# A four-layer graph network on one core: the last buckets of two layers by gathered rows, and fewer progress marks from TensorE

## The chip, the cores and the metric

The kernel runs on one core of a Trainium2 chip. The metric is device time in microseconds (us) of one execution. The program has four computing engines that run their own instruction streams: TensorE (PE, with its weight loads shown as PEld), VectorE (DVE), ScalarE (ACT) and GpSimd (POOL). A fifth stream, SyncE (SP), only issues transfers here. The engines know of one another only through semaphores: an instruction can add one to a semaphore when it is done (the code calls this a mark), and another engine can wait for a value.

## The reference

8192 nodes with 32 features each, 262144 edges sorted by their target node, four layers. Each layer adds a sum over incoming edges to the node's features and normalizes the result. `segment_sum` adds the rows of all edges with the same target.

```python
edge_index = jnp.stack([src, dst])
# layer 0: a 32x32 weight for each of 64 edge types
msg = einsum('ei,eio->eo', x[src], weight[etype]);  x = layernorm(x + segment_sum(msg, dst))
# layer 1: edge weight e
x = layernorm(x + segment_sum(x[src] * e[:, None], dst))
# layer 2
x = layernorm(x + segment_sum(x[src], dst))
# layer 3: a small network per edge makes four 8x8 matrices w from 32 edge features
h = relu(edge_feat @ W1 + b1);  w = (h @ W2 + b2).reshape(e, 4, 8, 8)
m = products of w with x[src] and 4 more edge features
x = layernorm(x + segment_sum(m, dst) + own part of x)
```

## The kernel before, in words

Edges are handled in tiles of 128 (one per partition), 2048 tiles in all. A group is 8 tiles (256 groups, `GG`), a quad is 4 tiles (512 quads, `NQ`). Nodes are handled in 64 blocks of 128 (`NB`), 8 blocks to a chunk for normalizing (`LC`). In the code `PE`, `V`, `A`, `G` and `S` are the five instruction streams; `X.mark(ins)` makes an instruction raise the engine's own semaphore, `X.after(...)` makes the engine wait. The order in each stream is the order of the Python code.

**Table.** First a table `fytab` of every node's row times each of the 64 weights is computed and stored to memory (line 408).

**Layer 0** (loop at `for g in range(GG + 2)`). For each group POOL gathers the 8 tiles' rows from `fytab` by indirect transfers (`gathers`, line 387, one transfer per tile, four after each half of the loop body). DVE builds a one-hot matrix of the target nodes (line 509) and splits the rows into three bf16 parts (lines 624 to 629, `parts`). PE multiplies both into a sum per window of nodes (line 662) and raises its mark. Four groups share one bank, which `bank_out` reduces (line 635). POOL fetches 12 groups ahead, and may start the next four gathers only when PE has marked the sums of the current group, and the four after that when PE has marked everything issued so far. When enough windows are ready, `windows` (line 499) and `normalize` (lines 458 to 468) produce eight blocks of new features, 8 times in the stage.

**Matrices, beside layer 0.** In the same loop `matrices(i)`, called 256 times, prepares layers 1 and 2: for 32 target nodes each call builds the columns of two dense adjacency matrices, one with edge weights (fp32, `famat`, 1 MB per call) and one with counts (bf16, `fcmat`, 0.5 MB). DVE builds one-hot matrices (lines 562, 564, 567). PE multiplies them for four units of eight nodes (line 576), each unit in two banks out of five, with a mark after every unit. ACT copies a unit's two banks to staging buffers (lines 581 and 582), which frees them. SP stores the staging buffers (lines 586 and 587) from two buffers in turn.

**Layers 1 and 2.** The matrices come back in 32 loads of 8 MB (layer 1, 2 blocks each) and 16 loads of 8 MB (layer 2, 4 blocks each) into two buffers (`bring`, line 698), each issued as one transfer when PE has marked the end of the multiplication with the buffer before. PE multiplies x with a load (lines 761 and 764), ACT copies the sums (line 770), and `turn` (line 741) folds them one load later and normalizes. `self_part` (lines 727 to 731) prepares layer 3's own part. At the end of layer 2 the rows are stored as the table `fxtab` (only there).

**Layer 3** (loop at `for q in range(NQ + LAG3 + 2)`). For each quad POOL gathers four tiles of rows from `fxtab`, eight quads ahead, each released by the mark of a quad's weights. PE computes the hidden values for two quads (line 899, `hidden`, with a mark; ACT applies relu in line 907), then the 4 x 256 weights of the quad (line 923, a mark), then the sums of the quad `LAG3` = 4 back (line 932, a mark). DVE makes the products (lines 960, 963, 967) from the weights' banks, of which there are two, builds a one-hot matrix (line 509) and reduces every second quad's sums (lines 988 to 991). Every other quad it also prepares factors (lines 863 to 870).

Of the kernel before, what the change touches and what calls it, by code (L numbers as in the profile page):

```python
# [12 lines left out]
FP = mybir.dt.float32  # L13
# [88 lines left out]
AW = 41200  # L102


@with_exitstack
def in_order(ctx: ExitStack, tc, x, a, w0, w1, b1, w2, si, keep):
# [8 lines left out]
    m["xtab"] = dram.tile([N, D], FP, name="fxtab")  # L115
# [30 lines left out]
def raw_layers(tc, x, a, w0, w1, b1, w2, si, m, bad):  # L146
# [7 lines left out]
    ytab, xtab, hist, amat, cmat = (m[k] for k in ("ytab", "xtab", "hist", "amat", "cmat"))  # L154
# [294 lines left out]
    x_st = Landing(tc, "st_x")  # L449
    ln_last = [None]  # L450

    def normalize(l, c, acc, pm, x_in, x_out, x3=None):


        ds = slice(c * LC, (c + 1) * LC)
        y, yc, sq = (lnf[:, k].rearrange("p (d f) -> p d f", f=D) for k in range(3))
        V.after(pm, ln_last[0])
        read = own(V, V.e.tensor_add(y, acc.rearrange("p (d f) -> p d f", f=D), x_in[:, ds, :]))  # L458
        own(V, V.e.tensor_reduce(lns[:, 0], y, AX.X, OP.add))
        own(V, V.e.tensor_scalar(lns[:, 1], lns[:, 0], 1.0 / D, None, op0=OP.mult))  # L460
        vm = V.mark(V.e.tensor_sub(yc, y, lns[:, 1, :, None].to_broadcast([P, LC, D])))
        A.after(vm)
        V.after(A.mark(A.e.activation(sq, yc, AF.Square)))
        A.after(V.mark(V.e.tensor_reduce(lns[:, 2], sq, AX.X, OP.add)))
        V.after(A.mark(A.e.activation(lns[:, 0], lns[:, 2], AF.Sqrt, bias=eps, scale=1.0 / D)))
        own(V, V.e.reciprocal(lns[:, 3], lns[:, 0]))
        xo = x_out[:, ds, :]
        ln_last[0] = V.mark(V.e.tensor_tensor(xo, yc, lns[:, 3, :, None].to_broadcast([P, LC, D]), op=OP.mult))
        if x3 is not None:

            r1, r2 = y, sq
            V.after(ln_last[0])
            own(V, V.e.tensor_copy(x3[:, ds, 0:D], xo))
            own(V, V.e.tensor_sub(r1, xo, x3[:, ds, 0:D]))
            own(V, V.e.tensor_copy(x3[:, ds, D:2 * D], r1))
            own(V, V.e.tensor_sub(r2, r1, x3[:, ds, D:2 * D]))
            ln_last[0] = V.mark(V.e.tensor_copy(x3[:, ds, 2 * D:], r2))
        if l == 2:
            S.after(ln_last[0])
            x_st.add(S.e.dma_start(xtab.rearrange("(d p) f -> p d f", p=P)[:, ds, :], xo))  # L480
        return read

    def windows(c, acc, free):

        d0 = c * LC
        todo = []
        for j in [0, 1, 2, 3, -2, -1, 4]:
            lo, hi = 0, LC
# [6 lines left out]
        wv = win.rearrange("p (d j) f -> p d j f", j=4)  # L495
        PE.after(*free)
        for n, (j, lo, hi) in enumerate(todo):
            g0 = 4 * (d0 + lo) + j
            ins = PE.e.matmul(acc[:, lo * D:hi * D].rearrange("p (d f) -> p d f", f=D),
                              shift[:, P - WS * j:2 * P - WS * j], wv[:, g0 // 4:g0 // 4 + hi - lo, g0 % 4, :],  # L500
                              start=(n == 0), stop=(n == len(todo) - 1))
        return PE.mark(ins)

    def ready(c):

        return min(GG, 4 * (LC * (c + 1) - 1) + 5)
# [41 lines left out]
    bank_free = {k: (acc_free[0] if k == 2 else None) for k in range(2, 7)}  # L548
    st_ld = [Landing(tc, f"st_m{k}") for k in range(2)]
    w_up = [None]  # L550
    units = [0]

    def matrices(i):
# [3 lines left out]
        if i % WB == 0:  # L557
# [6 lines left out]
        V.e.tensor_tensor(oh_l[:, b], iota[:, None, :].to_broadcast([P, 16, P]),  # L564
                          meta_l[:, pp, k0:k0 + 16, None].to_broadcast([P, 16, P]), op=OP.is_equal)
        wo = (i % WB) * 16
        vm = V.mark(V.e.tensor_tensor(oh_k[:, b, :, 1, :], oh_k[:, b, :, 0, :],
                                      w_ps[:, wo:wo + 16, None].to_broadcast([P, 16, 64]), op=OP.mult))
        PE.after(vm)
        for q in range(4):  # L570
            bk = [2 + (2 * units[0] + h) % 5 for h in range(2)]
            PE.after(*(bank_free[b5] for b5 in bk))
            for j in range(4):
                for h in range(2):
                    hs_ = slice(64 * h, 64 * h + 64)
                    ins = PE.e.matmul(bank[:, bk[h], :].rearrange("p (c s j) -> p c s j", s=64, j=4)[:, :, :, j],  # L576
                                      oh_l[hs_, b, 4 * q + j, :], oh_k[hs_, b, 4 * q + j], start=True, stop=True)
            pm = PE.mark(ins)
            A.after(pm, st_ld[b].mark() if q == 0 and st_ld[b].n else None)
            for h in range(2):  # L580
                A.e.activation(st_c[:, b, q, h], bank[:, bk[h], 0:256], AF.Copy)  # L581
                bank_free[bk[h]] = am = A.mark(A.e.activation(st_a[:, b, q, h], bank[:, bk[h], 256:512], AF.Copy))  # L582
            units[0] += 1
        oh_used[b] = pm
        S.after(am)
        st_ld[b].add(S.e.dma_start(amat[:, 2048 * i:2048 * (i + 1)], st_a[:, b].rearrange("p u h c -> p (u h c)")))
        st_ld[b].add(S.e.dma_start(cmat[:, 2048 * i:2048 * (i + 1)], st_c[:, b].rearrange("p u h c -> p (u h c)")))

# [4 lines left out]
    agg_free = [freed[0], freed[0]]  # L593
# [6 lines left out]
    per = 4  # L600
# [31 lines left out]
    def bank_out(n):  # L632

        V.after(sums_of[per * n + per - 1])
        agg_free[n % 2] = vm = V.mark(V.e.tensor_reduce(
            win[:, per * n:per * (n + 1), :], bank[:, n % 2, 0:per * 3 * D].rearrange("p (g c f) -> p g f c", c=3, f=D),
            AX.X, OP.add))
        return vm
# [5 lines left out]
    for g in range(GG + 2):  # L644
        if g >= 2 and (g - 2) % per == per - 1:
            vm = bank_out((g - 2) // per)
            while done < NB // LC and ready(done) <= g - 1:
                acc = bank[:, (g - 2) // per % 2, 0:LC * D]
                agg_free[(g - 2) // per % 2] = vm = normalize(0, done, acc, windows(done, acc, (vm,)), x_a, x_b)
                done += 1  # L650
        if g >= GG:
            continue
        h, bk, c = g % NO, (g // per) % 2, g % per
        if g == FIRST // 2:
            V.after(slots(), x_in)
        V.after(oh_free[h])
        one_hot(oh[:, h], g * GT, GT)
        PE.after(parts(g))
        if c == 0:
            PE.after(agg_free[bk])  # L660
        for t in range(GT):
            ins = PE.e.matmul(bank[:, bk, 3 * c * D:3 * (c + 1) * D], oh[:, h, t, :],  # L662
                              xp[:, g % 4, t].rearrange("p c f -> p (c f)"), start=(t == 0), stop=(t == GT - 1))
        oh_free[h] = sums_of[g] = PE.mark(ins)
        fetch_rows(g + AHEAD, 0, sums_of[g])
        if g >= FIRST:
            upto = min(CB, (g - FIRST + 1) * CB // (GG - FIRST - 4))
            while made < upto:
                matrices(made)
                made += 1  # L670
        fetch_rows(g + AHEAD, 1, now(PE))
# [9 lines left out]
    z = cut(NB, D)  # L681
    zx = cut(2, P)
    end = (now(PE), now(V), now(A), *stored)
# [5 lines left out]
    seq = [(1, c) for c in range(32)] + [(2, c) for c in range(16)]  # L689
    land = {}  # L690

    def bring(n):
        if n < len(seq):
# [3 lines left out]
            if l == 1:  # L697
                land[n] = m_ld[b].add(S.e.dma_start(buf[b], amat[:, c * 16384:(c + 1) * 16384]))
            else:
                land[n] = m_ld[b].add(S.e.dma_start(buf[b].bitcast(BF), cmat[:, c * 32768:(c + 1) * 32768]))  # L700

    bring(0)
    bring(1)
# [14 lines left out]
    own_part = [None]  # L718

    def self_part(j):  # L720
        xv = x_b[:, 4 * j:4 * j + 4, :].rearrange("p d f -> p (d f)")
        u = j % 2
        if j == 0:
# [5 lines left out]
        PE.after(A.mark(A.e.activation(zx[:, u], bank[:, 4 + u, 0:P], AF.Copy)), zf[1 - u])  # L729
        V.after(PE.mark(PE.e.matmul(bank[:, 6, 0:P], zx[:, u], sis, start=True, stop=True)))  # L730
        zf[u] = V.mark(V.e.tensor_add(z[:, 4 * j:4 * j + 4, :].rearrange("p d f -> p (d f)"), bank[:, 6, 0:P], xv))

    def turn(l, c, n, am):
# [10 lines left out]
        if d0 + nb == LC:  # L744
            out_free[o] = normalize(l, c * nb // LC, bank[:, 2 + o, 0:LC * D], pm, x_b if l == 1 else x_a,
                                    x_a if l == 1 else x_b, x3 if l == 1 else None)
            outs[0] += 1

    for n, (l, c) in enumerate(seq):
        b = n % 2  # L750
        nn = 256 if l == 1 else 512
        if n == 32:
            turn(*pend)
            pend = None
            PE.after(ln_last[0])
# [19 lines left out]
        if l == 2 and c >= 3 and c % 2 == 1:  # L775
            self_part(c - 3)
            self_part(c - 2)
# [3 lines left out]
    self_part(NB // 4 - 2)  # L781
    self_part(NB // 4 - 1)
# [19 lines left out]
    LAG3 = 4  # L802
# [23 lines left out]
    G.after(x_st.mark())  # L826
# [15 lines left out]
    def fetch_rows(q):  # L842

        if q < NQ:
            G.after(quad.get(q - AHEAD, {}).get("w"))
            rows[q // 2] = gathers(xtab, src, q // 8, q % 8 * 4, 4)
# [45 lines left out]
    def hidden(q):  # L892
# [9 lines left out]
        pm = PE.mark(ins)  # L902
        if q % 8 == 6:
            ef_free[k] = pm
# [9 lines left out]
    hidden(0)  # L914
    for q in range(NQ + LAG3 + 2):

        if q % 2 == 0 and q + 2 < NQ:
            hidden(q + 2)
        if q < NQ:
            k, wp = w_bank()  # L920
            PE.after(quad[q]["h"], w_free[k])
            for t in range(4):
                ins = PE.e.matmul(wp[:, t, :], hs[0:65, q % 4, t * P:(t + 1) * P], w2_s[0:65], start=True, stop=True)  # L923
            quad[q]["w"] = PE.mark(ins)
            quad[q]["k"] = k, wp
            fetch_rows(q + AHEAD)
# [544 lines left out]
```

## Time and profile before

| | us |
|---|---|
| median of 3 runs | 7502.81 (7498.84 to 7513.8) |
| the profiled execution | 7590.36 |
| its span, first to last instruction | 7588.5 |

The span by stage, each stage cut at the first or last instruction of its kind:

| stage | us | PE | DVE | ACT | POOL | PE clock | DMA share |
|---|---|---|---|---|---|---|---|
| table, start of layer 0 (0 to 435.6) | 435.6 | 186 | 118 | 165 | 214 | 0.63 | 0.56 |
| layer 0 and the matrices (to 3533.7) | 3098.1 | 1914 | 2097 | 1219 | 1816 | 0.67 | 0.55 |
| layers 1 and 2 (to 4521.0) | 987.3 | 581 | 55 | 37 | 0 | 0.77 | 0.98 |
| layer 3 (4531.2 to the end) | 3057.3 | 2725 | 2099 | 357 | 1943 | 0.90 | 0.12 |

The engine columns are busy microseconds, the clock is the share of full speed that TensorE was granted, and the DMA share is the mean busy share of the core's 16 DMA engines. A line of the timeline reads: start, length, engine, line of the kernel, instruction, what it writes and reads, count, and in brackets the idle time of the engine before it and what ended it. "Issue" there means that nothing in the profile ended it; "remote" means that a semaphore rose and the profile can't tell by whom. In the chain of waits, "DMA a<-b" is a transfer from its issue to its landing. The start of a matmul is recorded, while its end is modelled. Not every rise of a semaphore and not every matmul is in the record.

### The profile page before, as it was taken

To read this page: it belongs to the slowest core of one execution; us is meant where nothing else is said; L and a number is where in the kernel's file an instruction comes from. 1 tells how busy PE (TensorE), PEld (TensorE's weight loads), DVE (VectorE), ACT (ScalarE), POOL (GpSimd) and SP (SyncE) were. 2 spreads that over 40 slices of the span, in tenths; PEclk is the share of its full clock that TensorE was granted. 3 is DMA by queue.
4 is the path that set the end of the run, shared out by engine and by line. 5 is a ranking of instruction groups with operands and counts; after the bars stand their busy time and mean duration, and the time that the engine had idled before them with its cause. 6 is when DMAs were issued, how large, how long until landed. Compare 5 with 4: busy or idle time off the path is not lost.

```text
span 7588.5 us, 89476 instructions
## 1 busy us (share of the span) xinstructions
PE 5411.7 (71%) x34036; PEld 3845.9 (51%) x34036; DVE 4372.1 (58%) x9246; ACT 1780.4 (23%) x4886; POOL 3972.9 (52%) x4174
## 2 busy tenths in 40 slices
PE   7236566666666666665454778999998889889988
PEld 2125555555555555554222445555555555555555
DVE  3246666666666766665000016666767666676666
ACT  5224343333333443433000001111111111111110
POOL 3656565666565666651000006666666666666664
PEclk7556666666666666667777888989999998989898
DMA  9226555555555555557999971111111111111111
GB/s 350 87 67 146 136 144 137 150 136 144 142 139 143 144 150 136 146 135 265 432 431 431 393 303 21 24 24 24 24 24 24 24 24 24 24 24 24 25 24 21
DMA packets 290757, 999.52 MB, mean 132 GB/s; under 512 B 99022, under 2 KB 175887, under 8 KB 250639
## 3 DMA queue, kind: packets, MB, share of 16 engines
q1 hardware_dynamic: 155742, 916.89, 33.1%
q0 software_dynamic: 134144, 73.67, 9.4%
q8 instruction: 272, 4.46, 0.3%
q10 hardware_dynamic: 432, 3.15, 0.2%
q14 instruction: 167, 1.36, 0.1%
HBM read 521.39 MB, written 471.99 MB: 131 GB/s over the span
## 4 chain that ended last, share of the span: by engine, by line
PE 43%; another core or an unknown queue 17%; DVE 15%; DMA 10%; ACT 9%; issue 5%; POOL 1%; SPq 0%; DVEq 0%; ACTq 0%; POOLq 0%
PE bank L576 14%; PE bank L932 11%; PE bank L923 10%; DMA f_arena<-famat 6%; ACT f_arena L582 4%; ACT f_arena L581 4%; DVE f_arena L967 3%; DMA f_arena<-fcmat 3%; PE bank L899 2%; PE bank L761 2%; DVE f_arena L963 2%; DVE f_arena L509 2%; PE bank L764 2%; PE bank L408 1%
## 5 line engine op out<-in xcount | busy, mean ns | idle before, releaser
L387 POOL DMA_INDIRECT f_arena<-fxtab,f_src x2048 | 1942.9, 949 | 2132.7 <-PE bank L730 1077.1
L387 POOL DMA_INDIRECT f_arena<-fytab,f_row x2048 | 1961.8, 958 | 1286.5 <-issue 548.2
L576 PE MATMUL bank<-f_arena 64*128 64x128 f32 x16384 | 1626.3, 374 | 894.9 <-ACT f_arena L582 567.9
L576 PEld LDWEIGHTS bank<-f_arena 64*128 64x128 f32 x16384 | 1519.4, 280 | 989.5 <-ACT f_arena L582 477.4
L932 PE MATMUL bank<-f_arena 128*128 128x344 f32 x4096 | 1420.3, 491 | 28.6 <-issue 28.4
L923 PE MATMUL bank<-f_arena 65*128 65x256 f32 x4096 | 1107.2, 417 | 207.6 <-DVE f_arena L967 194.8
L581 ACT ACTIVATE f_arena<-bank 128x256 bf16<-128x256 f32 x2048 | 817.5, 399 | 1847.6 <-remote 1024.0
L923 PEld LDWEIGHTS bank<-f_arena 65*128 65x128 f32 x4096 | 808.2, 204 | 603.6 <-DVE f_arena L967 297.2
L932 PEld LDWEIGHTS bank<-f_arena 128*128 128x128 f32 x4096 | 856.3, 209 | 447.9 <-issue 149.0
L907 ACT ACTIVATE f_arena<-bank,f_arena 64x512 f32<-64x512 f32 x512 | 351.0, 686 | 2564.8 <-remote 1156.7
L582 ACT ACTIVATE f_arena<-bank 128x256 f32<-128x256 f32 x2048 | 828.6, 405 | 0.0
L562 DVE TENSOR_TENSOR f_arena<-bank,f_arena 128x1024 f32<-128x1024 f32 x256 | 313.3, 1224 | 806.2 <-remote 630.8
L509 DVE TENSOR_TENSOR f_arena<-bank,f_rel 128x512 f32<-128x512 f32 (+1 forms) x768 | 659.7, 859 | 139.9 <-ACT f_arena L541 127.9
L960 DVE TENSOR_TENSOR f_arena<-bank,f_arena 128x256 f32<-128x256 f32 x512 | 214.1, 418 | 836.6 <-remote 368.6
L564 DVE TENSOR_TENSOR f_arena<-bank,f_arena 128x2048 f32<-128x2048 f32 x256 | 586.6, 2291 | 8.8
L967 DVE TENSOR_TENSOR f_arena<-bank,f_arena 128x256 f32<-128x256 f32 x1536 | 550.7, 413 | 0.0
L761 PE MATMUL bank<-f_arena,f_x_b 128*32 128x256 f32 x4096 | 296.7, 461 | 332.6 <-DMA f_arena<-famat 332.6
L662 PE MATMUL bank<-f_arena 128*128 128x96 bf16 x2048 | 273.4, 261 | 364.8 <-issue 230.5
L662 PEld LDWEIGHTS bank<-f_arena 128*128 128x128 bf16 x2048 | 150.7, 120 | 484.4 <-issue 361.5
L761 PEld LDWEIGHTS bank<-f_arena,f_x_b 128*32 128x32 f32 x4096 | 146.2, 132 | 472.0 <-DMA f_arena<-famat 307.3
L458 DVE TENSOR_TENSOR f_lnf<-bank,f_x_b 128x256 f32<-128x256 f32 x8 | 3.4, 425 | 606.0 <-PE bank L741 606.0
L963 DVE TENSOR_TENSOR f_arena<-bank,f_arena 128x512 f32<-128x512 f32 x512 | 348.4, 681 | 0.0
(133 smaller groups left out, 3684.9 us busy)
## 6 DMA issues: line engine op xcount, KB each, us to landing
famat<-f_arena SPq DMA_DIRECT2D x256, 1024.0 KB
fcmat<-f_arena SPq DMA_DIRECT2D x256, 512.0 KB
fytab<-f_arena SPq DMA_DIRECT2D x64, 1024.0 KB
f_arena<-fytab,f_row POOLq DMA_INDIRECT x2048
f_arena<-fxtab,f_src POOLq DMA_INDIRECT x2048
f_arena<-laid_ea SPq DMA_DIRECT2D x64, 512.0 KB
f_arena<-laid_ea SPq DMA_DIRECT2D x64, 64.0 KB
f_arena<-laid_xT ACTq DMA_DIRECT2D x1, 1024.0 KB, 8.8
```

What stands on the lines that cost most here:

```text
L387: return G.e.indirect_dma_start(out=dest, out_offset=None, in_=table, in_offset=bass.IndirectOffsetOnAxis(ap=ix, axis=0))
L509: return V.e.tensor_tensor(o, iota[:, None, :].to_broadcast([P, n, P]), rel[:, t:t + n, None].to_broadcast([P, n, P]), op=OP.is_equal)
L564: V.e.tensor_tensor(oh_l[:, b], iota[:, None, :].to_broadcast([P, 16, P]), meta_l[:, pp, k0:k0 + 16, None].to_broadcast([P, 16, P]), op=OP ...
L576: ins = PE.e.matmul(bank[:, bk[h], :].rearrange("p (c s j) -> p c s j", s=64, j=4)[:, :, :, j], oh_l[hs_, b, 4 * q + j, :], oh_k[hs_, b, 4 ...
L581: A.e.activation(st_c[:, b, q, h], bank[:, bk[h], 0:256], AF.Copy)
L582: bank_free[bk[h]] = am = A.mark(A.e.activation(st_a[:, b, q, h], bank[:, bk[h], 256:512], AF.Copy))
L662: ins = PE.e.matmul(bank[:, bk, 3 * c * D:3 * (c + 1) * D], oh[:, h, t, :], xp[:, g % 4, t].rearrange("p c f -> p (c f)"), start=(t == 0), ...
L761: ins = PE.e.matmul(bank[q * D:(q + 1) * D, b, 0:256].rearrange("p (u h j) -> p u h j", h=2, j=4), x_b[:, s, :], mv[:, s], start=(s < 4), ...
L923: ins = PE.e.matmul(wp[:, t, :], hs[0:65, q % 4, t * P:(t + 1) * P], w2_s[0:65], start=True, stop=True)
L932: ins = PE.e.matmul(bank[:, g % 2, 0:MW], oh[:, c % NO, t, :], p[:, c % NP, t, :], start=(c % 2 == 0 and t == 0), stop=(c % 2 == 1 and t = ...
L963: V.e.tensor_tensor(pq[:, :, 0:128].rearrange("p t (o k) -> p t o k", k=16), wp[:, :, 0:128].rearrange("p t (o k) -> p t o k", k=16), a0[: ...
L967: ins = V.e.tensor_tensor(pq[:, :, 128 + 64 * mm:192 + 64 * mm].rearrange("p t (o i) -> p t o i", i=8), wp[:, :, 192:256].rearrange("p t ( ...
```

## The change

The change has these parts. Line numbers are those of the profile before.

1. **Gathered rows in layers 1 and 2.** The last 10 of 64 blocks of layer 1 and the last 4 of layer 2 (`HB`) are no longer computed from matrices. `matrices` is called 240 times in place of 256, and the last 24 of these build no `famat` part. The features after layers 0 and 1 are stored as tables too (`xtabs`; SP waits for `normalize`). In layer 1, 42 groups, and in layer 2, 18 groups of edges are gathered from these tables (`h_fetch`, at most four groups ahead, each waiting for the landing of the group two before), multiplied by the edge weight in layer 1, and summed through fp32 one-hot matrices (`h_sums`, two marks of PE per group). `h_turn` spreads them over the loads: after each load's multiplication it does the groups that are due, and calls `windows` and `normalize` for up to four blocks.
2. **Loads in pieces.** Layer 1 has 27 loads and layer 2 has 15. Each 8 MB load is issued as eight transfers of 1 MB.
3. **Fewer marks in layer 0.** `matrices` marks after every second unit, and units go through six banks (three pairs) in place of five. The mark for a group's sums is dropped where matrices follow: the first mark of `matrices` stands for both. POOL's first four gathers wait for that mark, the other four for the last. All groups use bank 0 for their sums, and a reduction after each group (`sums_out`, after the next group's one-hot and parts on DVE) takes the place of one for every four.
4. **One mark per quad in layer 3.** In each round PE does the hidden values, then the sums of the quad `LAG3` = 5 back, then the quad's weights, and marks once at the end. The hidden values' relu on ACT (`nonlinear`) waits for that mark.
5. The own part for layer 3 follows the blocks as they are finished, in whatever order.

```diff
+HB = {1: 10, 2: 4}
+MADE = {l: CB - 4 * HB[l] for l in (1, 2)}
...
-        if l == 2:
+        if l < 3:
             S.after(ln_last[0])
-            x_st.add(S.e.dma_start(xtab.rearrange("(d p) f -> p d f", p=P)[:, ds, :], xo))
+            x_st[l].add(S.e.dma_start(xtabs[l].rearrange("(d p) f -> p d f", p=P)[:, ds, :], xo))
...
+    def banks_of(u):
+        return [1 + (2 * u + h) % 6 for h in range(2)]
...
+            if q % 2 == 0:
+                continue
             pm = PE.mark(ins)
-            A.after(pm, st_ld[b].mark() if q == 0 and st_ld[b].n else None)
-            for h in range(2):
-                A.e.activation(st_c[:, b, q, h], bank[:, bk[h], 0:256], AF.Copy)
-                bank_free[bk[h]] = am = A.mark(A.e.activation(st_a[:, b, q, h], bank[:, bk[h], 256:512], AF.Copy))
-            units[0] += 1
+            marks.append(pm)
+            A.after(pm, st_ld[b].mark() if q == 1 and st_ld[b].n else None)
+            for u in range(2):
+                bk = banks_of(units[0] - 2 + u)
+                for h in range(2):
+                    ins = A.e.activation(st_c[:, b, q - 1 + u, h], bank[:, bk[h], 0:256], AF.Copy)
+                    if both:
+                        ins = A.e.activation(st_a[:, b, q - 1 + u, h], bank[:, bk[h], 256:512], AF.Copy)
+                    bank_free[bk[h]] = am = A.mark(ins)
...
+        if g:
+            agg_free = sums_out(g - 1)
...
+        PE.after(agg_free)
         for t in range(GT):
-            ins = PE.e.matmul(bank[:, bk, 3 * c * D:3 * (c + 1) * D], oh[:, h, t, :],
-                              xp[:, g % 4, t].rearrange("p c f -> p (c f)"), start=(t == 0), stop=(t == GT - 1))
-        oh_free[h] = sums_of[g] = PE.mark(ins)
-        fetch_rows(g + AHEAD, 0, sums_of[g])
+            ins = PE.e.matmul(bank[:, 0, 0:3 * D], oh[:, h, t, :], xp[:, g % 4, t].rearrange("p c f -> p (c f)"),
+                              start=(t == 0), stop=(t == GT - 1))
+        marks = []
         if g >= FIRST:
-            upto = min(CB, (g - FIRST + 1) * CB // (GG - FIRST - 4))
+            upto = min(MADE[2], (g - FIRST + 1) * MADE[2] // (GG - FIRST - 4))
             while made < upto:
-                matrices(made)
+                marks += matrices(made)
                 made += 1
-        fetch_rows(g + AHEAD, 1, now(PE))
+        if not marks:
+            marks.append(PE.mark(ins))
+        oh_free[h] = sums_of[g] = marks[0]
+        fetch_rows(g + AHEAD, 0, marks[0])
+        fetch_rows(g + AHEAD, 1, marks[-1])
...
+            for k in range(8):
+                o = buf[b][:, 2048 * k:2048 * (k + 1)]
+                if l == 1:
+                    land[n] = m_ld[b].add(S.e.dma_start(o, amat[:, c * 16384 + 2048 * k:c * 16384 + 2048 * (k + 1)]))
...
+    def h_fetch(l, g):
+        if g >= GG:
+            return
+        k = count["got"] % 4
+        count["got"] += 1
+        G.after(x_st[l - 1].mark() if g == HG[l] else None, hx_free[k], hl.get((l, g - 2), (0, None))[1])
+        for t in range(GT):
+            mk = h_ld[k].add(indirect(hx[:, k, t, :], xtabs[l - 1][:, :], src[:, g * GT + t:g * GT + t + 1]))
+        hl[l, g] = k, mk
...
+                V.after(hoh_free[r])
+                PE.after(V.mark(one_hot(hoh[:, r], g * GT + 4 * hh, 4)))
+                for t in range(4):
+                    ins = PE.e.matmul(bank[:, 6, (g - g0) * D:(g - g0 + 1) * D], hoh[:, r, t, :], hx[:, k, 4 * hh + t, :],
+                                      start=(hh == 0 and t == 0), stop=(hh == 1 and t == 3))
+                hoh_free[r] = hx_free[k] = PE.mark(ins)
+            h_fetch(l, g + 4)
...
+        h_turn(l, HG[l] + (GG - HG[l]) * c // (chunks[l] - 1))
...
-    LAG3 = 4
+    LAG3 = 5
...
-            quad[q]["w"] = PE.mark(ins)
             quad[q]["k"] = k, wp
-            fetch_rows(q + AHEAD)
...
+        if q < NQ + LAG3:
+            pm = PE.mark(ins)
+        if q < NQ:
+            quad[q]["w"] = pm
+            fetch_rows(q + AHEAD)
+        if 0 <= c < NQ:
+            quad[c]["a"] = pm
+        if q % 2 == 0 and q + 2 < NQ:
+            nonlinear(q + 2, pm)
```

## The prediction

> **What bounds the kernel now.** I read the page's group list first, then the idle times before POOL, then POOL, ACT, PE and DVE in order of time inside one group and one quad, and last the chain of waits through layers 1 and 2.
>
> ```profile
> span 7588.5 us, 89476 instructions
> ...
> L387 POOL DMA_INDIRECT f_arena<-fxtab,f_src x2048 | 1942.9, 949 | 2132.7 <-PE bank L730 1077.1
> L387 POOL DMA_INDIRECT f_arena<-fytab,f_row x2048 | 1961.8, 958 | 1286.5 <-issue 548.2
> ```
>
> No engine is full over the span, so the bound has to be found stage by stage. Two stages hold 4,096 gathers. In both, POOL goes through them at a fixed beat and then stops. Layer 0, POOL in order of time (start, length, instruction, idle before it in brackets):
>
> ```profile
> 2113.18 0.95 POOL L387 DMA_INDIRECT f_arena<-fytab,f_row  x1 [0.30 <-issue]
> 2114.43 0.94 POOL L387 DMA_INDIRECT f_arena<-fytab,f_row  x1 [0.30 <-issue]
> 2117.62 0.94 POOL L387 DMA_INDIRECT f_arena<-fytab,f_row  x1 [2.25 <-PE bank L662]
> ```
>
> The beat is 0.95 + 0.30 = 1.25 us. Eight gathers (one group, starts 2105.68 to 2114.43) are followed by a stop of about 2.25 us that a mark of PE ends: 8 x 1.252 + 1.92 more than the beat = 11.94 us per group. In layer 3 the same view shows 12 gathers (three quads) and a stop of 2.74: 17.4 us, 5.8 per quad. So POOL is the bound of both stages, plus a stop that waits for a mark of PE.
>
> Why do the marks keep POOL waiting? They come late. ACT (L581, L582 copy one unit out of its banks) and PE in the same group:
>
> ```profile
> 2106.09 4.58 PE L576 MATMUL bank<-f_arena 64*128 64x128 f32 x48 [0.41 <-ACT f_arena L582]
> 2113.66 2.08 PE L576 MATMUL bank<-f_arena 64*128 64x128 f32 x16 [2.99 <-issue]
> ```
>
> ```profile
> 2109.01 0.40 ACT L582 ACTIVATE f_arena<-bank 128x256 f32<-128x256 f32 x1
> 2112.86 0.38 ACT L581 ACTIVATE f_arena<-bank 128x256 bf16<-128x256 f32 x1 [3.44 <-remote]
> ...
> 2117.23 0.38 ACT L581 ACTIVATE f_arena<-bank 128x256 bf16<-128x256 f32 x1 [3.16 <-PE bank L576]
> ```
>
> Units one to three (48 matmul records) end by 2110.67. ACT begins the second at 2112.86 and the third at 2117.23, 6.6 us after its matmuls. In layer 3, PE's L923 of one quad ends at 5509.9 and DVE's L960, which waits for its mark, starts at 5517.04 after 5.33 us of idling. Between late marks lie about 4.3 us while POOL gathers, and several come at once when POOL has stopped. Where no gather is issued they are prompt: after the last layer 0 gather (3453.2) DVE runs without idling:
>
> ```profile
> 3457.39 1.22 DVE L562 TENSOR_TENSOR f_arena<-bank,f_arena 128x1024 f32<-128x1024 f32 x1
> 3465.47 1.22 DVE L562 TENSOR_TENSOR f_arena<-bank,f_arena 128x1024 f32<-128x1024 f32 x1
> 3473.57 1.22 DVE L562 TENSOR_TENSOR f_arena<-bank,f_arena 128x1024 f32<-128x1024 f32 x1
> ```
>
> That is 8.09 us per group against 11.94. Likewise layer 3's last quads (7527.9 to 7537.2) take 4.65 each, PE without a pause. Layers 1 and 2 are bound by their loads:
>
> ```profile
> 3657.35 9.74 PE bank L761 x128
> 3667.11 28.87 DMA f_arena<-famat
> ...
> 4206.62 16.79 PE bank L764 x64
> 4223.42 26.43 DMA f_arena<-fcmat
> ```
>
> Layer 1's DMA share is 1.00 at 430 GB/s; PE works about 9.5 of 19.3 us per chunk there, and 16 of 21.6 in layer 2.
>
> **Part 1: fewer marks (layers 0 and 3).** What can be won is POOL's stops. Layer 0: from the first gather after the prefetch (435.6) to the last (3453.2) are 3018 us for 1920 gathers, 1920 x 1.252 = 2404 of them at the beat: 614 us of stops. Layer 3: 4531.2 to 7528.8 are 2998 us for 2048 gathers, 2564 at the beat: 434.
>
> A rule that speaks against counting on this: the Trainium skill's TensorE page ("TensorE: Matmul & The Clock Gate", "The cost: per-tile semaphore tail") gives an increment 26.3 ns. The change drops about 3 of 5 per group and 1.5 of 2.5 per quad, 244 x 3 + 512 x 1.5 = 1500, an estimate of 40 us by the rule. The row above has a mark late by 6.6 us and POOL stopped 2.25 us per group, so I go by the row: the limit is 1048 us.
>
> Layer 0 new: marks m0 (sums and units 0, 1) and m1 (units 2, 3). POOL waits for m0 before its first four gathers and m1 before the other four. With one late mark per 4.3 us the two need 8.6 us, under POOL's 10.0. The new loops: unit 3 needs ACT's four copies of unit 0, 0.27 us apart, so 1.1 us after m0 arrives; with six banks that is short. DVE now stops for m0(g-1) in sums_out(g-1), ahead of the one-hots of g (L562, L564, L567: 4.7 us), and PE's sums of g wait for sums_out (single bank 0). That loop is 0.2 + 4.7 + about 3.1 (32 of the 48 records in 4.58) + lateness, 8 us plus up to 4.3. DVE's own work is 8.09 + about 0.3 for a reduction per group in place of one per four. Ends: 10.0 (POOL alone) and 12.3 (every m0 fully late). I take 10.5, near POOL's row, as a mark early in a streak comes promptly (unit one here). 240 x 10.5 + the 80 us now between the last gather and the first load = 2600; the start (a mark kept from 457.7 to 486.2 there) is left, 30 us: 2630 against 3098, **-470**. The 16 dropped calls of matrices spare the groups that now make two; they and the lighter last 24 calls sit inside this. x_st stores of layer 0 make SP wait seven times for normalize, behind them the stores of the next matrices: cover is two buffers, a group; nothing, at most 7 x 8 = 56 us without it.
>
> Layer 3 new: hidden, sums of q-5, weights of q, one mark. PE's free pace is 4.65, DVE's 4.02, POOL's 5.01; one mark per 5 us against 4.3 possible. Hidden's ACT (two of 0.69) now waits to the end of PE's round, but its result is wanted a round later, and sums with lag 5 take values from two rounds earlier. Ends: 5.01 and 5.86 (now). I take 5.2: 512 x 5.2 + 60 = 2722 against 3057, **-335**.
>
> **Part 2: gathered rows (layers 1 and 2).** Removed: 5 of 32 and 1 of 16 loads of 8.39 MB: 352 for 402.7 MB, at 430 GB/s 117 us. Added: 60 groups x 8 gathers of 1.25 = 600 us of POOL, which idled 1077 us here. A gather's 1 KB packets take 0.10 us of each DMA engine in layer 3 and 0.22 beside layer 0's stores: 480 x 0.10 to 0.22 = 48 to 106 us of a full DMA. PE gets 16 matmul records per group at about 0.2 us (the 128-column fp32 weight loads of L741 take 0.19), 3.3 us, 1.6 groups per layer 1 chunk (5 us into 9.8 of slack), 1.3 per layer 2 chunk (4 into 5). DVE, nearly idle here, gets about 1.8 us per group. In turn marks become late here too: in layer 2 a late matmul mark holds back the next load on SP. The last store of x1 for layer 2's gathers queues on SP behind loads: 10 to 40 us once. The cut of each 8 MB load into eight is the second rule against the change: "DMA: Bandwidth & Descriptors", "Measured", has 1 MB at 341 GB/s and 16 MB at 425, which would be 1032 against 828 us for 352 MB, a loss of 200. But those are lone transfers; here eight queue at once. The row: packets of 8 KB (layer 0 stores) took 0.32 us, those of 64 KB 2.43, 408 against 432 GB/s: at worst 47 us. Sum: -117 + 77 + 20 (queue) + 0 to 47, between -60 and +80; I take **-20**.
>
> **Sum.** 7588.5 - 470 - 335 - 20 = 6763 us of span. The profiled execution (7590.4) stands 1.2% over the median 7502.8, so 6763 x 0.9885 = **6685 us**.
>
> **Rivals.** (a) POOL streams, PE's marks get later the longer the streak (one kept 28 us at 457.7), so half of the stops stay: (470 + 335) / 2 + 20 = 423, **7085**. For it: that first streak. Against: steady streaks of 12 gathers still let one through per 4.3 us. (b) The marks' number doesn't matter, only POOL: the rule's 40 us, about 90 for the double groups, 20 in part 2: **7355**. Against: the waits go through marks. (c) Slower: POOL, now tied to both marks, stops before each four gathers of layer 0: 2 x (5.01 + 1.92) = 13.9 against 12.57 on average (3018 / 240): +310, with layer 3 unchanged and part 2 at +80: 7978 x 0.9885 = **7890**. It decides from 1.3 stops per group. For it: m1 follows m0 by only one copy and one unit. Against: POOL has five microseconds of work in which m1, due after three, can arrive.
>
> **Chances.** Forecast 0.60, (a) 0.20, (b) 0.08, (c) 0.10, no change 0.02, so faster 0.88, slower 0.10. The forecast's own range is 6430 (all stops gone, part 2 at -60) to 6900; to leave no more than 2 in 10 out, 6420 to 7200. No change means within 0.2%, 15 us.
>
> **What would show it.** Right: POOL in runs of far over 12 gathers; groups at 10 to 10.8 us, quads at 5.0 to 5.3; POOL's share above 65%; layers 1 and 2 at 930 to 1030 us. Wrong: POOL idling behind PE twice per group, DVE idle before its new L635 reduction, or PE idle in layer 2 behind gathered rows.

## The result and the profile after

The changed kernel takes **7784.49 us** (median of 4 runs, 7780.85 to 7797.27) against 7500.83 for the kernel before: 1.0378 times as long, interval 1.036 to 1.0396. Forecast were 6685 us. Its profiled execution took 7797.27 us; the page begins so, and its group list has the two kinds of gathers so:

```profile
span 7795.6 us, 88905 instructions
...
L389 POOL DMA_INDIRECT f_arena<-fxtab,f_src x2528 | 2400.7, 950 | 1965.1 <-issue 705.4
L389 POOL DMA_INDIRECT f_arena<-fytab,f_row x2048 | 1957.9, 956 | 1210.3 <-issue 530.9
```

The gathers of layer 0 still leave POOL idle for 1210 us (1286 before). The stages, each from its first matmul to that of the next ("between" runs from the last matmul of layer 2 to the first of layer 3):

| us | to layer 1 | layer 1 | layer 2 | between | layer 3 |
|---|---|---|---|---|---|
| before | 3558.9 | 627.6 | 334.5 | 15.0 | 3052.5 |
| after | 3483.3 | 856.7 | 378.9 | 30.2 | 3046.5 |
| difference | -76 | +229 | +44 | +15 | -6 |

The sum, +207, is the difference of the spans. Two places differ from the forecast: layer 1 grew, and the stops did not go. By the prediction's own sum (first gather to last, less 1.252 us for each) POOL's stops fell from 614 to 531 us in layer 0 and from 434 to 425 in layer 3. First layer 3, all engines in order of time:

```profile
5493.21 1.89 PE L1041 MATMUL bank<-f_arena 65*128 65x256 f32 x8
...
5495.22 0.94 POOL L389 DMA_INDIRECT f_arena<-fxtab,f_src  x1 [0.30 <-issue]
...
5497.26 1.89 PE L1041 MATMUL bank<-f_arena 65*128 65x256 f32 x8
5498.43 0.43 DVE L1077 TENSOR_TENSOR f_arena<-bank,f_arena 128x256 f32<-128x256 f32 x1 [3.54 <-remote]
...
5498.66 0.94 POOL L389 DMA_INDIRECT f_arena<-fxtab,f_src  x1 [2.50 <-remote]
```

The weights that carry the mark end at 5495.10. DVE and POOL go on at 5498.43 and 5498.66, after 3.54 and 2.50 us of idling, while PE is already in the next quad's weights. There is one mark per quad now, and it is still late. Layer 1, then layer 2, in a table by stretches, of the kernel before and of the changed one:

```profile
core 0: us, PE busy (x) PEld busy (x) DVE busy (x) ACT busy (x) POOL busy (x), PEclk, DMA share, GB/s
3558.90:4186.50 627.60, 314.68 (x4225) 162.86 (x4226) 33.78 (x96) 18.92 (x48) 0.00 (x0) 0.73 1.00 431
4186.50:4521.00 334.50, 266.32 (x1175) 149.94 (x1175) 21.07 (x62) 18.06 (x41) 0.00 (x0) 0.89 0.93 372
```

```profile
3483.30:4340.00 856.70, 393.59 (x4297) 248.65 (x4297) 109.39 (x274) 17.85 (x47) 292.68 (x309) 0.66 0.97 273
4340.00:4719.00 379.00, 310.25 (x1360) 192.41 (x1360) 40.66 (x100) 16.69 (x39) 135.98 (x144) 0.82 0.82 316
```

In layer 1 the DMA engines are as full as before (0.97), yet move 273 GB/s in place of 431.

One thing is needed to read the experiments: the same kernel before took 7493 to 7516 us in some jobs, this comparison among them (**held** below), and 6429 to 6457 us in others (**free**), so each run is compared with the kernel before of its own job.

### The profile page after: what moved, and what is told of

Read it like the earlier page. It is cut to its first block, busy times and chain, and to the rows that moved or that the text cites. A ratio compares the mean times of both kernels' runs of the same rounds, so it can differ in the third digit from the quotient of the medians.

```text
span 7795.6 us, 88905 instructions
## 1 busy us (share of the span) xinstructions
PE 5668.1 (73%) x33318; PEld 4078.5 (52%) x33318; DVE 4389.5 (56%) x9596; ACT 1627.3 (21%) x4438; POOL 4426.6 (57%) x4654
## 4 chain that ended last, share of the span: by engine, by line
PE 46%; another core or an unknown queue 20%; DVE 10%; issue 8%; DMA 8%; ACT 6%; SPq 2%; POOL 0%; DVEq 0%; ACTq 0%; POOLq 0%
PE bank L592 16%; PE bank L1035 11%; PE bank L1041 7%; DMA f_arena<-famat 7%; PE bank L871 3%; PE bank L1007 2%; SPq L732 2%; PE bank L868 2%; ACT f_arena L1017 2%; DVE f_arena L576 2%; ACT f_arena L604 1%; ACT f_arena L602 1%; PE bank L682 1%; PE bank L410 1%
## 5 line engine op out<-in xcount | busy, mean ns | idle before, releaser
L389 POOL DMA_INDIRECT f_arena<-fxtab,f_src x2528 | 2400.7, 950 | 1965.1 <-issue 705.4
L592 PE MATMUL bank<-f_arena 64*128 64x128 f32 (+1 forms) x15360 | 1879.1, 396 | 860.5 <-issue 575.9
L592 PEld LDWEIGHTS bank<-f_arena 64*128 64x128 f32 x15360 | 1650.3, 292 | 1073.0 <-issue 754.3
L1035 PE MATMUL bank<-f_arena 128*128 128x344 f32 x4096 | 1504.6, 516 | 239.9 <-DVE f_arena L1106 131.0
L517 DVE TENSOR_TENSOR f_arena<-bank,f_rel 128x512 f32<-128x512 f32 (+1 forms) x888 | 738.2, 835 | 466.5 <-PE bank L824 293.9
L1041 PE MATMUL bank<-f_arena 65*128 65x256 f32 x4096 | 987.3, 384 | 7.3 <-issue 7.3
L604 ACT ACTIVATE f_arena<-bank 128x256 f32<-128x256 f32 x1728 | 717.1, 415 | 0.0
L658 DVE TENSOR_REDUCE f_arena<-bank 128x32 f32<-128x96 f32 x256 | 65.9, 257 | 881.9 <-remote 443.9
L576 DVE TENSOR_TENSOR f_arena<-bank,f_arena 128x2048 f32<-128x2048 f32 x240 | 549.8, 2291 | 8.2
L1007 PE MATMUL bank<-f_arena 32*64 32x512 f32 x1024 | 286.2, 635 | 72.3 <-ACT f_arena L1017 68.6
L682 PE MATMUL bank<-f_arena 128*128 128x96 bf16 x2048 | 190.3, 260 | 144.0 <-issue 57.5
```

Source lines behind the costliest of these rows:

```text
L389: return G.e.indirect_dma_start(out=dest, out_offset=None, in_=table, in_offset=bass.IndirectOffsetOnAxis(ap=ix, axis=0))
L517: return V.e.tensor_tensor(o, iota[:, None, :].to_broadcast([P, n, P]), rel[:, t:t + n, None].to_broadcast([P, n, P]), op=OP.is_equal)
L576: vm = V.mark(V.e.tensor_tensor(oh_l[:, b], iota[:, None, :].to_broadcast([P, 16, P]), meta_l[:, pp, k0:k0 + 16, None].to_broadcast([P, 16 ...
L604: ins = A.e.activation(st_a[:, b, q - 1 + u, h], bank[:, bk[h], 256:512], AF.Copy)
L1007: ins = PE.e.matmul(bank[64 * h:64 * h + 64, 2, :], w1_s[r * D:(r + 1) * D, :], ef[r * D:(r + 1) * D, k, (q % 8) // 4, :], start=True, sto ...
L1035: ins = PE.e.matmul(bank[:, g % 2, 0:MW], oh[:, c % NO, t, :], p[:, c % NP, t, :], start=(c % 2 == 0 and t == 0), stop=(c % 2 == 1 and t = ...
```

## The experiments

**The change taken apart (a free job, before 6433.69 us).** Of the changed kernel: the loads as one transfer again; and, besides that, no gathered rows (`HB = 0`), so that only the rarer marks are left. Of the kernel before: only the cut into eight.

```diff
 # e1_one_load, e3_marks_only: bring()
-            for k in range(8):
-                o = buf[b][:, 2048 * k:2048 * (k + 1)]
...
+                land[n] = m_ld[b].add(S.e.dma_start(buf[b], amat[:, c * 16384:(c + 1) * 16384]))
 # e3_marks_only also
-HB = {1: 10, 2: 4}
+HB = {1: 0, 2: 0}
 # e2_split_only: the eight pieces of the change in the kernel before
```

> The changed kernel with each load of layers 1 and 2 as one transfer of 8 MB again, gathered rows kept. Theory (the cut into eight pieces of 8 KB per partition lowers the loads from 430 to about 270 GB/s): layer 1 moves at 400 to 430 GB/s again, layers 1 and 2 take 900 to 980 us in place of about 1250, the whole about 7450 to 7530 us. Rival (the gathered rows take the bandwidth): layer 1 stays under 330 GB/s and the whole stays above 7680 us.

> The kernel before with nothing but the loads of layers 1 and 2 cut into eight pieces. Theory (the pieces): 268 MB of layer 1 at 270 GB/s are 994 us in place of 620, layer 2 about 400 in place of 350, the whole about 7900 us. Rival (the gathered rows): no difference, 7500 us within 40. Third (what the prediction had, packets of 8 KB only 5% slower): 7550 us.

> The changed kernel without gathered rows in layers 1 and 2 (all buckets are matrices again) and with each load as one transfer: only the rarer marks of layers 0 and 3 are left of the change. Theory (PE's marks are late because POOL streams gathers, whatever their number): layer 0 about 3070 and layer 3 about 3040 us as in the changed kernel, the whole 7450 us within 50. Rival (the prediction: fewer marks remove the stops, and something of the gathered rows undid that): about 6700 us, or at least under 7100.

Measured: e1 6605.61 us (1.0255, 1.0233 to 1.0277), e2 6692.21 (1.0419, 1.0387 to 1.0452), e3 6446.92 (1.0019, 1.0011 to 1.0026). The expectations reckon with 7500 us for the kernel before; the differences count. The pieces alone cost 258 us: the first theory of e2, at a smaller price (layer 1 862.6 us, 994 expected). The rarer marks alone bring nothing here, but in a free job POOL hardly stops in layer 0, so there was little to gain; e10 below asks again in a held one. In e1 the rival came near: layer 1 took 757 us at 318 GB/s, though not for want of bandwidth, as the DMA share was 0.81. Its order of time shows why:

```profile
3203.32 0.42 DVE L815 TENSOR_TENSOR f_arena<-f_arena 128x256 f32<-128x256 f32 x1 [22.52 <-DMA f_arena<-fxtab,f_src]
...
3204.40 3.62 PE L822 MATMUL bank<-f_arena 128*128 128x32 f32 x16 [20.46 <-DVE f_arena L517]
```

DVE waits 22.5 us for rows that lie in the DMA engines behind packets of 64 KB (2.60 us each), PE behind it 20.5 us, and behind PE the next load. So the pieces were there for the gathers' sake.

**Fewer gathers in layer 3.** In e4 (same job) every second gather of the changed kernel was left out; in e8 the same in the kernel before.

```diff
         for t in range(t0, t0 + n):
+            if table is xtabs[2] and t % 2:
+                continue
```

> The changed kernel with every second gather of layer 3 left out (those rows are stale; marks, matmuls and DVE's work are all kept). Theory (the gathers make PE's marks late): DVE finds PE's marks promptly, PE runs without a pause, a quad takes about 4.65 us as in the tail of layer 3, layer 3 about 2430 us, the whole about 7180 us. Rival (the marks are late for a reason of PE's own): DVE still idles 3 us or more before its L1077 every second or third quad, a quad takes above 5.5 us, the whole stays above 7650 us.

> The kernel before, with its more numerous marks, and every second gather of layer 3 left out (those rows are stale). On a chip where the marks are late, theory (gathers make them late): a quad takes about 4.65 us in place of 5.8, layer 3 about 2430 us in place of 3057; rival (PE's own): above 2950 us. On a chip where the marks are prompt: layer 3 about 2470 us in place of 2615, as PE then bounds it in place of POOL, and the number of marks costs nothing (the changed kernel with half of its gathers took 2470).

Both fell into free jobs, where marks are prompt: layer 3 took 2470 us with the changed kernel's marks and 2443 with those of before, against about 2620 with all gathers. So a free layer 3 is bound by POOL's beat, with PE close behind, and rarer marks win nothing. Of late marks these two tell nothing.

**The changed kernel again, and the distance between rows (a free job, before 6450.25 us).** A row of the matrix of layer 1 lies 2 MB from that of the next partition. e6 and e7 move them apart:

```diff
-    m["amat"] = dram.tile([P, NU * 512], FP, name="famat")
-    m["cmat"] = dram.tile([P, NU * 512], BF, name="fcmat")
+    m["amat"] = [dram.tile([P, NU * 256 + 1024], FP, name=f"famat{k}") for k in range(2)]
+    m["cmat"] = dram.tile([P, NU * 512 + 2048], BF, name="fcmat")
```

> The changed kernel itself beside the kernel before, as the first four experiments met a chip where the kernel before takes 6434 us and POOL does not stop. If PE's marks are prompt there too: layers 0 and 3 within 20 us of the kernel before, layers 1 and 2 about 1150 to 1200 us in place of 980, ratio 1.025 to 1.035. If the marks are late: 7780 us to 7500 as in the first comparison.

> The changed kernel, gathered rows and eight pieces kept, but the matrices of layer 1 lie in two tensors with 1 MB + 4 KB from one partition's row to the next in place of 2 MB, those of layer 2 with 1 MB + 4 KB in place of 1 MB. Theory (the pitch slows the pieces of 8 KB): their packets in layer 1 take about 330 ns in place of 460, layer 1 550 to 620 us in place of 800 to 860, the whole 200 to 250 us below the changed kernel and below the kernel before. Rival (their size slows them): packets stay above 420 ns, the whole stays within 40 us of the changed kernel.

> The kernel before with the loads in eight pieces and the same padded rows, no gathered rows. Theory (pitch): layer 1 at 400 GB/s or more, 635 to 680 us, against 863 with pieces alone; the whole within 50 us of the kernel before. Rival (size of the pieces): layer 1 stays above 800 us, the whole 200 us or more above the kernel before.

Measured: e5 6717.03 us (1.0415, 1.0398 to 1.0433), e6 6438.44 (0.9982, 0.9975 to 0.9989), e7 6451.17 (1.0002, 0.9993 to 1.0011). Layer 1 by stretches, of e2, e7, e5 and e6 in this order:

```profile
2854.90:3717.50 862.60, 313.65 (x4224) 162.94 (x4224) 33.74 (x96) 18.89 (x48) 0.00 (x0) 0.67 1.00 314
```

```profile
2849.00:3494.70 645.70, 313.67 (x4225) 162.58 (x4225) 33.78 (x96) 18.91 (x48) 0.00 (x0) 0.72 1.01 419
```

```profile
2862.00:3713.00 851.00, 367.59 (x4297) 239.29 (x4297) 109.66 (x274) 17.84 (x47) 292.68 (x308) 0.66 0.97 275
```

```profile
2850.00:3438.20 588.20, 372.67 (x4296) 242.12 (x4296) 109.50 (x274) 17.85 (x47) 302.15 (x318) 0.71 1.02 400
```

The pieces have the same size in all four; the new distance alone brings 314 to 419 and 275 to 400 GB/s. A piece's packet of 8 KB took 415 ns in e2 and 315 in e7, beside gathers 458 in e5 and 327 in e6. So the distance slows pieces of this size, and not their size alone. And in a free job the changed kernel loses 267 us, nearly as much as in the first comparison (284), with layers 0 and 3 within 15 us of those in e7, where they are the kernel before's.

**Quarters of layers 0 and 3.** One kernel holds four tests: a quarter as it is; one with more marks that nobody waits for (the expectation says three to five times as many; it is 7 times in layer 3 and 13 in a call of `matrices`); one with every second gather left out; one with a POOL memset (0.82 us) in its place. s2 has 12 blocks of layer 1 by rows and none of layer 2, s3 also no padding.

```diff
+            kind = part(s * WT + t)
+            if kind < 2 or t % 2 == 0:
...
+            elif kind == 3:
+                G.after(now(G))
+                G.mark(G.e.memset(arena[:, end0:end0 + 850], 0.0))
```

> The changed kernel with padded rows, whose layers 0 and 3 are each four quarters: as it is; with three to five times as many marks of PE, for which nobody waits; with every second gather left out; with every second gather replaced by a memset of about the same length on POOL (the rows left out are stale). Where PE's marks are late, if gathers make them late, whatever the number of marks: quads of layer 3 about 5.8, 5.8, 4.65 and 4.65 to 5.1 us, groups of layer 0 about 11.9, 11.9, 8.1 to 9, at most 10; if their number does it: the second quarter is slower than the first by 1 us per quad or more; if a busy POOL does it, without DMA: the fourth quarter stays at 5.8. Where the marks are prompt: quads 5.0, 5.0, 4.65 and 5.0 us and groups 10.0, 10.0, 8.1 to 8.5 and 10.0 us.

> The same four quarters of layers 0 and 3 as in s1_parts (as it is; three to five times the marks; every second gather left out; those replaced by memsets on POOL, the rows left out being stale), now with 12 buckets of layer 1 by rows and none of layer 2, run for a chip on which the kernel before takes about 7500 us. There: if gathers make the marks late, quads 5.8, 5.8, 4.7, 4.7 to 5.1 us; if the number of marks does, the second quarter is above 6.5; if a busy POOL does, the fourth stays at 5.8. On a chip with prompt marks: 5.0, 5.0, 4.7, 4.7 us as in s1_parts, layers 1 and 2 about 900 us, the whole about 6110 us.

> s2_parts with the padding taken out: the matrices of layer 1 in two tensors at exactly 1 MB from row to row, those of layer 2 at exactly 1 MB as in the changed kernel; quarters of layers 0 and 3 as in s2_parts (every second gather of the last two quarters left out, rows stale). Theory (any row distance that is a large power of two slows pieces of 8 KB, 2 MB more than 1 MB): packets of layer 1 between 350 and 420 ns, layer 1 600 to 720 us against 578 with padding. Rival (only 2 MB does): 330 ns and 575 to 590 us. On a chip where the kernel before takes 7500 us the quarters tell as in s2_parts: gathers 5.8, 5.8, 4.7, 4.7 to 5.1 us a quad; number of marks: second quarter above 6.5; busy POOL: fourth at 5.8.

s1 and s2 ran free (6172 us beside 6441, 6150 beside 6435), s3 held (6984 beside 7497). A quad of layer 3 took, quarter by quarter:

| us per quad | as it is | more marks | half the gathers | memsets for them |
|---|---|---|---|---|
| s1_parts, free | 5.0 | 5.0 | 4.7 | 4.7 |
| s3_pitch, held | 5.8 | 5.8 | 4.7 | 4.7 |

Groups of layer 0 in s3, from the sums of one to those of the next inside each quarter: 12.3, 11.9, 8.7, 8.4 us. DVE's waits in s3 for the weights' mark (L1097 is its first product; total, times, longest), in the second and then the third quarter:

```profile
DVE f_arena L1097 <- PE bank L1059: 170.6, 57, 6.1
```

```profile
DVE f_arena L1097 <- PE bank L1059: 62.1, 109, 0.8
```

Many more marks change nothing. Without every second gather the longest wait falls from 6.1 to 0.8 us and the hold is gone, and a POOL that is busy with memsets instead does not bring it back. Gathers in close sequence do it, and not the marks. Of the row distance s3 says less than hoped: packets took 343 ns at exactly 1 MB against 329 with padding (s2), nearer the rival, so most of the loss belongs to 2 MB; but its layer 1 took 809 us, and there PE was the bound.

**A version from this.** 12 blocks of layer 1 by rows, none of layer 2, padded rows:

```diff
-HB = {1: 10, 2: 4}
+HB = {1: 12, 2: 0}
```

> The changed kernel with padded rows, 12 buckets of layer 1 by gathered rows in place of 10, none of layer 2, loads in eight pieces. Theory (each gathered bucket of layer 1 is worth about 6 us once the pieces move at full rate, those of layer 2 cost more than they spare): layer 1 about 575 us in place of 588, layer 2 about 325 in place of 346 and its end 15 in place of 30, the whole 40 to 55 us below the changed kernel with padded rows, ratio to the kernel before 0.988 to 0.993. Rival (gathers of 12 buckets bound layer 1 through POOL, and matrices of layer 2 lengthen layer 0): ratio 0.998 or more.

It took 6375.97 us in a free job, 0.9897 of the kernel before (0.988 to 0.9913), as expected: layer 1 577.3, layer 2 319.7 us. Does it hold where PE is held, and what are the marks alone worth there? Both kernels again, in one job:

> Only the rarer marks of layers 0 and 3, again, for a job in which the kernel before takes about 7500 us (PE held up by gathers). There: layers 1 and 2 as in the kernel before, layer 0 about 76 us and layer 3 about 6 us shorter as in the changed kernel, the whole about 7420 us, 1% below the kernel before. In a job in which the kernel before takes 6434 us: 6447 us as in e3_marks_only.

> The version of e9_best again, for a job in which the kernel before takes about 7500 us. There: gathers hold PE in layer 1, which takes about 800 us as in s3_pitch in place of 628, layers 0 and 3 gain about 80 us, the whole 7560 to 7620 us and slower than the kernel before. Rival (the padded rows are worth the same there): about 7350 us. In a job with 6434 us for the kernel before: 6376 us as in e9_best.

The job was a held one (before 7503.64). The marks alone: 7556.95 us, 1.008 (1.0056 to 1.0104), so a loss where I expected a gain of 1%. The new version: 7686.6, 1.0246 (1.0203 to 1.0288), slower than expected. So it beats both kernels only in free jobs. Its layer 1, held and then free:

```profile
3489.90:4301.60 811.70, 564.01 (x4295) 307.59 (x4296) 122.58 (x295) 17.46 (x46) 362.02 (x383) 0.69 0.74 285
```

```profile
2845.50:3422.80 577.30, 373.80 (x4294) 251.48 (x4294) 123.64 (x295) 17.42 (x46) 361.68 (x383) 0.73 1.02 396
```

The same instructions on the same data keep PE busy for 564 us in place of 374, and the DMA engines wait for it (0.74).

## Why the prediction was wrong, point by point

- **POOL's beat** (1.25 us) was the same in all runs, and in free jobs POOL alone bounds layer 0: in e5 2009 gathers of layer 0 follow one another without a pause of 1.5 us. The forecast's free paces were right: 10.0 us per group against 9.8 to 9.9, 5.01 per quad against 5.0.
- **"What can be won is POOL's stops", by fewer marks: this step failed.** I read "between late marks lie about 4.3 us" as a rate at which marks can pass, so that fewer marks would all be in time. The groups took 12.2 us (10.5 forecast), the quads 5.8 (5.2), and s3 shows the same pace with many times the marks. What holds the pace is the gathers themselves: without every second one the stops are gone. I had the right observation on the page, that marks are prompt wherever no gather is issued, and drew no conclusion about the gathers from it. PE's waits show what was exchanged, before, then after (total, times, longest):

```profile
PE bank L576 <- ACT f_arena L582: 567.9, 356, 29.2
...
PE bank L576 <- issue: 277.7, 96, 5.3
PE bank L662 <- issue: 230.5, 426, 9.3
```

```profile
PE bank L592 <- issue: 575.9, 856, 4.2
...
PE bank L592 <- ACT f_arena L604: 188.5, 105, 8.3
...
PE bank L682 <- issue: 57.5, 11, 13.4
```

  Before the matrices' matmuls (L576, now L592) the wait for free banks fell by 380 us, and PE's unexplained "issue" idle rose by 298, of which 173 came from the group sums (L662, now L682). In the free e5 PE has no "issue" row at all, and the same matmuls keep it busy for 1348 us in place of 1879: in held jobs PE itself is held. I had shown such a row (2.99 us of "issue" before L576) and not asked what it was.
- **The skill's rule of 26.3 ns per increment**, cited in the prediction (the page has it for the tail of matmuls packed in tiles), gave 40 us where my row gave 805. The rarer marks alone cost 13 us free and 53 held. The rule was nearer, though it says nothing of gathers.
- **Part 2, -20 us: the term for packets of 8 KB (0 to 47 us) failed.** e5 against e6 puts it at 263 us in layer 1 (851.0 less 588.2). I took 0.32 us from stores; loads of the same size at the same row distance take 415 ns alone and 458 beside gathers. The skill's rule that I set aside (1 MB at 341 GB/s, +200 us) came near the right price by luck: it blames the size of the transfer, which e7 excludes. Another section of the same page fits better: the Trainium skill, "DMA: Bandwidth & Descriptors", "Latency and other measured facts", has copies from memory to memory with rows of 16 KB fall as the distance of the rows grows through powers of two, to 164 GB/s at 2 MB, and 4 KB of padding restore the rate at 4 MB. Here 8 KB pieces went from 314 to 419 GB/s. It is not the distance alone either: loads of 64 KB per row moved 431 at the same 2 MB.
- **The gathers' share of part 2 (77 us) was right**: padded, e6 against e7 cut to the same number of loads: 588 - 646 x 27/32 = 43 us in layer 1, and 346 - 322 x 15/16 = 44 in layer 2 (e7's layer 2 took 322 us). That PE's part of it stays hidden was true only in free jobs. In held ones gathered rows bring the hold into layer 1, which had no gathers before: 812 us even with padded rows (e11). In the first comparison layer 1 took 857 us with slow packets, so both bounds probably lie close together and the slow packets hide the other.
- **Rivals.** (a), that marks get later the longer POOL streams, has the streaks of the last section on its side, but the stops did not halve: 1048 us became 956. (b), that the marks' number doesn't matter, was right in its mechanism and lacked the price of part 2. (c) was slower for a reason that did not come: layer 0 became 76 us shorter in the profiled runs. Part of that may be the profiled run of before, 88 us above its median: against medians, the marks cost 53 us, and the rest of the loss, 7784 - 7557 = 227 across two held jobs, is part 2. That (c)'s 7890 lies nearest is luck.

What stays open: where in the kernel the 53 us lie, since the one trace of before in such a job is of its longer run; what makes a job a held one (not the chip, of which the expectations speak: number 12 had a free job and a held one); and by what way gathers reach PE.

## What to carry to other kernels

When an engine is late, ask whether it is late with its message or with its work, and vary the suspected cause (here the gathers) before the thing that suffers (the marks). Take a packet's time from a row of the same direction, size and address pattern, and pad a matrix whose rows lie a large power of two apart before cutting its loads. Work moved into a stage brings its side effects along: ask what held the stage that it comes from.

## What the runs showed of the hardware that was not expected

**PE's matmuls start further apart while POOL streams gathers, in some jobs.** The matmuls of one load of layer 1 (64, which the profile records as 128) have no wait and no mark among them. Parts of two loads' matmuls in the changed kernel's trace, in order of time, the first beside no gather:

```profile
3709.38 8.85 PE L868 MATMUL bank<-f_arena,f_x_b 128*32 128x256 f32 x128 [14.98 <-DMA f_arena<-famat]
...
3930.73 5.68 PE L868 MATMUL bank<-f_arena,f_x_b 128*32 128x256 f32 x47 [9.20 <-DMA f_arena<-famat]
3937.43 0.38 PE L868 MATMUL bank<-f_arena,f_x_b 128*32 128x256 f32 x1 [1.02 <-issue]
...
3940.93 0.38 PE L868 MATMUL bank<-f_arena,f_x_b 128*32 128x256 f32 x1 [1.00 <-issue]
3941.64 6.54 PE L868 MATMUL bank<-f_arena,f_x_b 128*32 128x256 f32 x77 [0.33 <-issue]
```

POOL gathers from 3919.9 to 3939.6. After some 16 us of that PE gets on by single matmuls with 1 us between them; soon after the last gather it runs 77 in 6.54 us. Over all loads, the mean time from one matmul's start to the next, sorted by the gathers started in the 4 us before it: in e11 (held) 91 ns with none and 254 with three; the same kernel in e9 (free) 72 and 68. The length of the stream counts: with at most 6 gathers in the 20 us before, e11 has 79 ns, with 14 or more 645 (e9: 66 and 68). Where layer 1 has no gathers at all, a held job is as fast as a free one: 70 ns in the first profile and in e2. This is the hold, and the late marks of the first profile are PE's own lateness as well as its messages'.

Three other causes don't fit. The granted clock was 1.00 from 3936.5 to 3941.6, amid the single matmuls. Slow gather packets don't do it: in e11's layer 0, with padded rows, they took 101 ns, and a group still took 12.2 us. And the packets that bring instructions took 1.06 us in e11's layer 1 and 1.07 in e9's.

**One program, two paces.** The kernel before took 6434 us free and 7500 held, 17% more, with POOL's beat of 1.25 us the same in both; the mean granted clock of TensorE was lower where PE was held (0.767 in e10, 0.852 for the same kernel in e3). Whether the lower clock follows from the hold or has a part in it is not shown, but it is too little to be the cause: in layer 1 of e11 and e9 the clock was 0.69 and 0.73, and PE was busy 564 and 374 us.

**Row distance.** Loads of 8 KB per partition with rows 2 MB apart moved 314 GB/s, with 1 MB + 4 KB between them 419; stores of 8 KB to the same rows hardly changed (330 ns a packet in e5's layer 0, 324 in e6's). Small packets beside them did: padding took stores of 4 KB from 227 to 170 ns and the gathers' packets of 1 KB from 227 to 102. So the 0.22 us that the prediction read for gathers "beside layer 0's stores" belongs to the row distance. Layer 0 is no shorter for it (its DMA share fell from 0.61 to 0.46).
